# Two match buffers in layer 1 of a graph attention kernel, with other counts of one-hot and weighted-row buffers

## The chip, the cores and the metric

The kernel runs on one core of one Trainium2 chip. A core has a matrix engine (TensorE, PE in the profile, with its weight loads shown as PEld), three engines for element-wise work (VectorE or DVE, ScalarE or ACT, GpSimd or POOL) and a queue engine for transfers (SyncE or SP). The metric is the device time of one execution in microseconds (us); lower is better.

## The reference, cut to what matters

A pre-normalised residual block around a two-layer graph attention network, on 6250 nodes and 100000 edges that are sorted by destination. A loop from each node to itself is added to the edges.

```python
def gat_conv(x, src, dst, W, a_src, a_dst, bias, heads):
    h = (x @ W).reshape(n, heads, -1)
    alpha_s = (h * a_src[None]).sum(-1)
    alpha_d = (h * a_dst[None]).sum(-1)
    e = leaky_relu(alpha_s[src] + alpha_d[dst], 0.2)
    e = exp(e - segment_max(e, dst)[dst])
    alpha = e / (segment_sum(e, dst)[dst] + 1e-16)
    return segment_sum(h[src] * alpha[:, :, None], dst).reshape(n, -1) + bias

h = relu(layernorm(x))                          # 6250 x 768
h = relu(gat_conv(h, src, dst, W1, ..., heads=4))   # 256 features
h = relu(gat_conv(h, src, dst, W2, ..., heads=1))   # 256 features
return x + relu(h @ Wm1 + bm1) @ Wm2 + bm2      # 768 features
```

## The kernel before, in words

**Stages.** Nodes are cut into NT = 49 tiles of 128, edges into 784 tiles of 128 (782 of them with real edges). A first stage normalises x and forms the features of layer 1, one node tile after another; each row (268 numbers: four heads of 64 features and a one, and eight exponentials of the scores) stays in SBUF as `kept[t]` and is also stored to a table in DRAM. Then the edges of layer 1 are worked through, and then those of layer 2, both by the function `layer_edges`. The work after layer 2 (the two dense layers and the residual) is woven into layer 2's loop.

**The loop over groups.** `layer_edges` runs over NG = 196 groups of four edge tiles. The order on every engine is written by hand: each engine runs its own instructions in the order in which the Python code issues them, and waits on semaphores where it must. In group g of layer 1 stand, in this order:

- `gather(g + 8)`: POOL issues one indirect DMA for each of the four tiles (L652). It brings the 128 source rows of the tile into half of a buffer `G`, which holds a pair of tiles. There are 20 such buffers, taken in turn.
- `pair(g, 0)`: DVE forms the weights of a pair in PSUM (`factors`, L730 and L740), and multiplies the gathered rows by them into a buffer `hw` (L742). That is the last read of `G`. PE then multiplies the one-hot matrix `hot` of each tile with `hw` and adds up in PSUM (`o_ps`, L754), two groups to one sum.
- `make_hot(g + 1)`: DVE writes the one-hot matrices of the next group (L680) in a buffer of the pool `eg`.
- in every fourth group pieces of node work, masks and their products with the prepared numbers `win` (L698).
- the matches, see below; then `pair(g, 1)`, and in every second group `take_sum`, in which DVE takes a finished `o_ps` of groups up to g - 4 (L771).

**The matches.** The edges' first rows are needed while the table is still being stored. For 23 pairs of tiles (list `SOON`) the gather ran early, against the part of the table that was there; rows of later nodes are put in afterwards by a product. `soon_hits` has DVE compare the 128 source numbers of a tile with the last m node tiles, m from 2 to 20 (`soon_hit`, 128 x 128m, L379). `soon_missing` has PE multiply them with the rows `kept` (m products, each two records in the profile, L389). `soon_out` has ACT copy the result from PSUM (L395), and `soon_whole` adds it to the row. There are 46 of these, k = 0 to 45: the hits of k stand in group 8i + 1 for k = 2i and in group 8i + 5 for k = 2i + 1, the product two groups after for even k and one after for odd k. Before the change all 46 share one buffer, since the pool `pre1` has one buffer for each name.

**Buffers that bind the engines.** `hot` has 5 buffers, one for each group. `hw` has 10 in layer 1, one for each pair of tiles. `o_ps` has 3 in PSUM.

**Preparing.** `prepare` runs once ahead of each layer: from the scores of all nodes it forms `win` and `own`, with seven arrays in between (`rho`, `parts`, `r1`, `r2`, `e1`, `e2`, `v`). In layer 1 it takes them from the pool `pre1`, which stays open for the whole layer.

Of the kernel before, what the change touches and what calls it, by code (L numbers as in the profile page):

```python
# [10 lines left out]
F32 = mybir.dt.float32  # L11
BF16 = mybir.dt.bfloat16
# [5 lines left out]
P = 128  # L18
# [9 lines left out]
NT = -(-N // P)  # L28
NQ = 4 * NT
TPG = 4  # L30
NG = NQ
# [24 lines left out]
SOON_FROM, SOON_HELD = min(SOON), 16  # L56
# [14 lines left out]
def kernel(  # L71
# [266 lines left out]
    soon_G, soon_of, soon_p, soon_hit, soon_m = {}, {}, {}, {}, {}  # L338
# [34 lines left out]
    def soon_hits(pool, k):  # L373

        i, t = divmod(k, 2)
        if i < len(SOON):
            m = NT - SOON[i]
            soon_hit[k] = pool.tile([P, NT - SOON_FROM, P], F32, name="soon_hit")
            nc.vector.tensor_tensor(  # L379
                soon_hit[k][:, :m],  # L380
                soon_of[i][:, t * P:(t + 1) * P].unsqueeze(1).to_broadcast([P, m, P]),
                nid_ps[:, SOON[i]:].unsqueeze(2).to_broadcast([P, m, P]), ALU.is_equal)
# [178 lines left out]

    def prepare(wk, layer, H):

        s, d = sd[layer][:, :, :H], sd[layer][:, :, H:]
        rho = wk.tile([P, NT, H], F32, name="rho")
        nc.scalar.activation(rho, d, AF.Exp, scale=SLOPE - 1.0)
        parts = wk.tile([P, NT, H, 3], BF16, name="parts")
        nc.vector.tensor_copy(parts[:, :, :, 0], rho)
        r1 = wk.tile([P, NT, H], F32, name="r1")
        nc.vector.tensor_sub(r1, rho, parts[:, :, :, 0])  # L570
        nc.vector.tensor_copy(parts[:, :, :, 1], r1)
        r2 = wk.tile([P, NT, H], F32, name="r2")
        nc.vector.tensor_sub(r2, r1, parts[:, :, :, 1])
        nc.vector.tensor_copy(parts[:, :, :, 2], r2)

        win = wk.tile([P, NG + 4, 3 * H], BF16, name="win")
        pv = parts.rearrange("p n h k -> p n (h k)").unsqueeze(2)
        for q in range(4):
            r = slice(32 * q, 32 * q + 32)
            to = win[r, q:q + NG].rearrange("p (n j) k -> p n j k", j=4)  # L580
            of = pv[r].to_broadcast([32, NT, 4, 3 * H])
            if q % 2:
                nc.scalar.activation(to, of, AF.Copy)
            else:
                nc.vector.tensor_copy(to, of)
        nc.vector.memset(win[64:96, 0:2], 0.0)
        nc.vector.memset(win[96:128, 0:3], 0.0)
        nc.vector.memset(win[0:32, NG:NG + 4], 0.0)
        e1 = wk.tile([P, NT, H], F32, name="e1")
        nc.scalar.activation(e1, s, AF.Exp)  # L590
        e2 = wk.tile([P, NT, H], F32, name="e2")
        nc.scalar.activation(e2, s, AF.Exp, scale=SLOPE)
        v = wk.tile([P, NT, H], F32, name="v")
        nc.vector.tensor_mul(v, e2, rho)
        own = wk.tile([P, NT, H], F32, name="own")
        nc.vector.tensor_max(own, v, e1)
        nc.vector.tensor_reduce(flags[:, layer - 1:layer], sd[layer].rearrange("p n k -> p (n k)"),
                                AX.X, ALU.max, apply_absolute_value=True)
        return SimpleNamespace(win=win, own=own)
# [24 lines left out]
    def layer_edges(layer, H, node, pre, matched, pre_pool):  # L624
# [1 line left out]


        C = HID // H
        with tc.tile_pool(name=f"eg{layer}", bufs=5) as eg, \
                tc.tile_pool(name=f"hw{layer}", bufs=10 if layer == 1 else 14) as hwp, \  # L630
                tc.tile_pool(name=f"sum{layer}", bufs=4) as sums, \
                tc.tile_pool(name=f"sm{layer}", bufs=4) as sm:
            G, hot, e_ps, o_ps = {}, {}, {}, {}
# [231 lines left out]
            for g in range(NG):  # L865
# [39 lines left out]
                if layer == 1:  # L905
                    for i, at in enumerate(SOON_GROUP):
                        for k, hits_at in ((2 * i, at - 10), (2 * i + 1, at - 6)):
                            if g == hits_at + 3 + (k % 2 == 0):
                                soon_out(sm, k)
                            if g == at - 1:  # L910
                                soon_whole(G, k)
                            if g == hits_at:
                                soon_hits(pre_pool, k)
                            if g == hits_at + 1 + (k % 2 == 0):
                                soon_missing(k)
                        if g == at - 13:
                            soon_sources(pre_pool, i)
# [41 lines left out]
    with tc.tile_pool(name="w2p", bufs=1) as wp, tc.tile_pool(name="wk2", bufs=2) as wk:  # L959
# [51 lines left out]
        with tc.tile_pool(name="pre1", bufs=1) as pre:  # L1011
            pre1 = prepare(pre, 1, 4)
            layer_edges(1, 4, Node1(), pre1,
                        lambda: scores_in(ps, w2, *w2_in, KH, 1, "parts", 1), pre)


    with tc.tile_pool(name="wmp", bufs=1) as wp, tc.tile_pool(name="x3", bufs=4) as xp, \
# [10 lines left out]
        def matched():  # L1028

            vars(pre2).update(vars(prepare(pre, 2, 1)))  # L1030
            nc.scalar.dma_start(wm1, Wm1.rearrange("(k p) f -> p k f", p=P))
            nc.scalar.dma_start(wm2, Wm2.rearrange("(k p) f -> p k f", p=P))
            with nc.allow_non_contiguous_dma(reason="256 numbers"):
                nc.scalar.dma_start(bm1c, bm1.rearrange("(k p) -> p k", p=P))
            nc.scalar.dma_start(bm2r, bm2_d)
            nc.vector.memset(ones_r, 1.0)
# [120 lines left out]
        for stage in range(2):  # L1157
            first_hits(pre, 2, stage)
        layer_edges(2, 1, Node2(), pre2, matched, pre)

    edges_stack.close()
# [310 lines left out]
```

## Time and profile before

| what | value |
|---|---|
| median of 3 runs (lowest, highest) | 2555.83 us (2548.58, 2555.97) |
| the profiled execution's own time, and its span | 2560.77 us, 2559.0 us |
| first stage, 0 to 185 us of the span | PE busy 151.19, DVE 121.57, POOL 86.99 us |
| layer 1, 185 to 1345 us | PE 791.57, DVE 720.89, ACT 154.09, POOL 701.70 us |
| between the layers, 1345 to 1436 us | PE 50.35, DVE 43.22, POOL 38.37 us |
| layer 2, 1436 us to the end | PE 792.12, DVE 507.75, POOL 705.50 us |
| mean granted PE clock | 0.793 |
| mean duration of a gather (L652), of a `soon_hit` (L379), of `hw` in layer 1 (L742), of `hot` (L680) | 956, 1640, 695, 682 ns |

Busy time of an engine is the sum of the durations of its instructions; waiting for a semaphore is not in it. PE and PEld overlap, and the ends of matmuls are modelled. The page puts idle time down to what ended it: "remote" or "another core or an unknown queue" is an event for which the profile knows no instruction, and "issue" is time for which it knows no wait. With one core there is no other core, so both leave something untold. L numbers are lines of the kernel before; in the kernel after they are 5 to 7 higher from `prepare` on.

### The profile page before, as it was taken

How to read it: one execution, taken by the hardware profiler on the slowest of the kernel's cores; microseconds unless marked ns; L12 is line 12 of the kernel's file. 1: busy time of each engine (PE TensorE's matmuls, PEld its weight loads, DVE VectorE, ACT ScalarE, POOL GpSimd, SP SyncE). 2: the span in 40 equal slices, each digit the busy share in tenths (PEclk: the TensorE clock that was granted, in tenths of full speed). 3: DMA queues.
4: the chain of work that ended last, by engine and by line, in shares of the span. 5: the costliest groups of instructions: out<-in, count | busy, mean ns of one | idle time of the engine just before them, and what ended most of it. 6: DMA issues, size and time to landing. Idle time of an engine off the chain costs nothing.

```text
span 2559.0 us, 26651 instructions
## 1 busy us (share of the span) xinstructions
PE 1785.2 (70%) x7728; PEld 1282.6 (50%) x7729; DVE 1393.4 (54%) x4195; ACT 442.2 (17%) x1368; POOL 1532.6 (60%) x1666
## 2 busy tenths in 40 slices
PE   9952758667768667767766566676767767776677
PEld 7741546555546445545554344454444444444445
DVE  7742566666667667666666444444444434444444
ACT  6640111111111111111112011111111111111112
POOL 5257465565666666666554566666666666666661
PEclk9985778788778778878878677777878777777778
DMA  9986345545545555555444445545554454545542
GB/s 353 334 272 218 104 136 144 151 131 147 156 134 155 147 142 160 138 155 157 127 117 122 126 121 157 148 137 153 155 154 148 137 154 139 157 145 153 150 148 78
DMA packets 167326, 400.35 MB, mean 156 GB/s; under 512 B 36631, under 2 KB 54254, under 8 KB 167174
## 3 DMA queue, kind: packets, MB, share of 16 engines
q0 software_dynamic: 75072, 211.10, 31.0%
q1 hardware_dynamic: 90732, 185.99, 21.2%
q10 hardware_dynamic: 1370, 1.48, 0.2%
q8 instruction: 65, 1.06, 0.2%
q14 instruction: 87, 0.71, 0.1%
HBM read 333.87 MB, written 64.56 MB: 156 GB/s over the span
## 4 chain that ended last, share of the span: by engine, by line
PE 40%; issue 24%; DVE 15%; another core or an unknown queue 11%; POOL 5%; DMA 4%; ACT 1%; SPq 0%; DVEq 0%; POOLq 0%; ACTq 0%
PE o_ps L754 20%; PE y_ps L1124 6%; POOL G L652 5%; PE missing L389 5%; PE h_ps L452 4%; DVE hw L742 3%; DMA G<-table,src_i 3%; DVE hot L680 3%; DVE factors L740 2%; DVE factors L730 2%; DVE acc L771 1%; PE tp L1114 1%; DVE hw L737 1%; PE e_parts L698 1%
## 5 line engine op out<-in xcount | busy, mean ns | idle before, releaser
L652 POOL DMA_INDIRECT G<-table,src_i x1507 | 1440.7, 956 | 851.8 <-issue 376.3
L754 PE MATMUL o_ps<-G,hw 128*128 128x258 f32 x1564 | 525.2, 462 | 231.3 <-issue 187.3
L754 PE MATMUL o_ps<-hw,hot 128*128 128x260 f32 x1564 | 476.0, 441 | 161.1 <-issue 125.3
L754 PEld LDWEIGHTS o_ps<-G,hw 128*128 128x128 f32 x1564 | 350.6, 231 | 375.9 <-issue 279.7
L754 PEld LDWEIGHTS o_ps<-hw,hot 128*128 128x128 f32 x1564 | 327.1, 217 | 271.5 <-issue 164.4
L389 PE MATMUL missing<-kept,soon_hit 128*128 128x268 f32 x1028 | 265.2, 406 | 71.1 <-issue 70.1
L737 DVE TENSOR_SCALAR hw<-iota_ps,dcol,w 128x128 f32<-128x128 f32 x782 | 284.9, 406 | 16.3 <-DVE w L733 2.0
L742 DVE TENSOR_TENSOR hw<-G,factors 128x520 f32<-128x520 f32 x391 | 271.9, 695 | 22.0 <-DVE factors L740 6.4
L780 ACT ACTIVATE sum<-acc 32x260 f32<-32x260 f32 (+1 forms) x384 | 160.0, 417 | 689.5 <-DVE acc L771 263.5
L389 PEld LDWEIGHTS missing<-kept,soon_hit 128*128 128x128 f32 x1028 | 201.5, 198 | 123.2 <-issue 88.7
L1128 DVE TENSOR_TENSOR y<-y_ps,xt 128x384 f32<-128x384 f32 (+1 forms) x98 | 54.5, 556 | 271.1 <-PE o_ps L754 91.8
L1124 PE MATMUL y_ps<-wm,mT 128*128 128x384 f32 x392 | 181.5, 593 | 13.0 <-ACT mT L1119 8.7
L680 DVE TENSOR_TENSOR hot<-iota_ps,dcol 128x512 f32<-128x512 f32 x196 | 133.6, 682 | 104.2 <-remote 97.2
L379 DVE TENSOR_TENSOR soon_hit<-soon_of,iota_ps 128x1408 f32<-128x1408 int32 (+18 forms) x46 | 75.4, 1640 | 210.2 <-remote 140.2
L452 PE MATMUL h_ps<-w,r 128*128 128x264 f32 (+1 forms) x588 | 141.3, 395 | 19.4 <-ACT r L442 10.8
L698 PE MATMUL e_parts<-win,mask 128*128 128x12 bf16 (+1 forms) x1564 | 70.2, 168 | 116.7 <-issue 116.0
L452 PEld LDWEIGHTS h_ps<-w,r 128*128 128x128 f32 x588 | 110.5, 195 | 42.9 <-ACT r L442 12.9
L730 DVE TENSOR_TENSOR factors<-G,factors 128x8 f32<-128x8 f32 (+1 forms) x782 | 125.0, 160 | 7.1 <-DVE acc L771 2.6
L698 PEld LDWEIGHTS <-mask 128*128 128x128 bf16 x1564 | 62.7, 99 | 130.8 <-issue 122.0
L1124 PEld LDWEIGHTS y_ps<-wm,mT 128*128 128x128 f32 x392 | 77.8, 221 | 88.2 <-issue 48.1
L1119 ACT ACTIVATE mT<-tp,bm1c 128x128 f32<-128x128 f32 x98 | 30.6, 363 | 508.5 <-PE o_ps L754 305.7
L771 DVE SCALAR_TENSOR_TENSOR acc<-acc,keep,o_ps 128x260 f32<-128x260 f32 (+1 forms) x192 | 91.3, 475 | 11.7 <-PE o_ps L754 8.3
(418 smaller groups left out, 1281.4 us busy)
## 6 DMA issues: line engine op xcount, KB each, us to landing
xt<-in_x SPq DMA_DIRECT2D x96, 384.0 KB
drow<-dmod_d SPq DMA_DIRECT2D x49, 512.0 KB
mask_d<-mask SPq DMA_DIRECT2D x97, 256.0 KB
mask<-mask_d SPq DMA_DIRECT2D x97, 256.0 KB
G<-table,src_i POOLq DMA_INDIRECT x1507
xTt<-in_xT SPq DMA_DIRECT2D x49, 384.0 KB
out<-y SPq DMA_DIRECT2D x48, 384.0 KB
table<-kept SPq DMA_DIRECT2D x49, 134.0 KB
```

The lines of the kernel that those rows point to most:

```text
L389: nc.tensor.matmul(soon_p[k], hit[:, T - there], kept[T], start=(T == there), stop=(T == NT - 1))
L452: nc.tensor.matmul(h_ps[:, :n], r[:, k], w1[:, k, :n], start=(k == 0), stop=(k == KI - 1))
L652: nc.gpsimd.indirect_dma_start(out=G[k // 2][:, k % 2], out_offset=None, in_=table[layer], in_offset=bass.IndirectOffsetOnAxis(ap=src_i[:, ...
L680: nc.vector.tensor_tensor(hot[g][:, T[0]:T[0] + n], iota_ps.unsqueeze(1).to_broadcast([P, n, P]), dcol[:, k:k + n].unsqueeze(2).to_broadca ...
L698: nc.tensor.matmul(parts[t][:, at + k], m[:, k * P:(k + 1) * P], pre.win[:, 2 * u + 2], start=True, stop=True)
L730: nc.vector.tensor_mul(v, e2, rho)
L737: nc.vector.tensor_scalar(hw[:, t], iota_ps, dcol[:, k:k + 1], w[:, t], ALU.is_equal, ALU.mult)
L742: nc.vector.tensor_mul(hw, Gp[:, :, :RW[1]].rearrange("p t (h c) -> p t h c", h=H), w.unsqueeze(3).to_broadcast([P, 2, H, C + 1]))
L754: nc.tensor.matmul(o_ps[u], l, r[:, :RW[layer]], start=(g % 2 == 0 and k == 0), stop=(g % 2 == 1 and k == tiles(g)[-1]))
L771: nc.vector.scalar_tensor_tensor(acc, run[0], keep[:, u % 2:u % 2 + 1], o_ps.pop(u), ALU.mult, ALU.add)
L780: nc.scalar.activation(done[t][r], acc[r], AF.Copy)
L1124: nc.tensor.matmul(y_ps, mT[:, j], wm2[:, j, s * half:(s + 1) * half], start=False, stop=(j == KH - 1))
```

## The change

`soon_hit` gets two buffers in turn. `hot` gets 6 buffers instead of 5 (the pool `eg` is opened with 6 in layer 2 too, where nothing is taken from it). `hw` gets 8 in layer 1 instead of 10. `prepare` takes `win` and `own` from the pool that stays, and everything else from a pool of its own that is closed when `prepare` ends, so its room goes to the pools opened after it.

```diff
-            soon_hit[k] = pool.tile([P, NT - SOON_FROM, P], F32, name="soon_hit")
+            soon_hit[k] = pool.tile([P, NT - SOON_FROM, P], F32, name="soon_hit", bufs=2)
...
     def prepare(wk, layer, H):
 
+        win = wk.tile([P, NG + 4, 3 * H], BF16, name="win")
+        own = wk.tile([P, NT, H], F32, name="own")
+        with tc.tile_pool(name=f"prep{layer}", bufs=1) as tmp:
+            return prepared(tmp, layer, H, win, own)
+
+    def prepared(wk, layer, H, win, own):
+
         s, d = sd[layer][:, :, :H], sd[layer][:, :, H:]
...
-        win = wk.tile([P, NG + 4, 3 * H], BF16, name="win")
...
-        own = wk.tile([P, NT, H], F32, name="own")
...
-        with tc.tile_pool(name=f"eg{layer}", bufs=5) as eg, \
-                tc.tile_pool(name=f"hw{layer}", bufs=10 if layer == 1 else 14) as hwp, \
+        with tc.tile_pool(name=f"eg{layer}", bufs=6) as eg, \
+                tc.tile_pool(name=f"hw{layer}", bufs=8 if layer == 1 else 14) as hwp, \
```

In bytes of a partition, a `soon_hit` takes 10240, a `hot` 2048, an `hw` 2080, and the seven arrays of `prepare` in layer 1 together 5880.

The order of the instructions on every engine is the same in both kernels. What differs is the semaphores that some wait for: in the kernel after, no `soon_hit` waits for PE, 158 of the `hot` no longer do, and 362 of the `hw` of layer 1 wait for PE where they waited for DVE alone. `rho` at the head of `prepare` waits for other queues.

## The prediction

> **What bounds the kernel now.** I read the page's head, then the windows by stage, then who waits in layer 1, then the timelines of POOL, DVE and PE over a few periods.
>
> ```profile
> span 2559.0 us, 26651 instructions
> ...
> 185.00:1345.00 1160.00, 791.57 (x3567) 600.04 (x3568) 720.89 (x1860) 154.09 (x535) 701.70 (x731) 0.80 0.52 147
> ...
> 1436.00:2559.00 1123.00, 792.12 (x3292) 528.39 (x3291) 507.75 (x1907) 165.52 (x437) 705.50 (x742) 0.77 0.48 143
> ```
>
> Columns: stretch, length, busy us (and count) of PE, PEld, DVE, ACT, POOL, then granted clock, DMA share, GB/s. The change can act in layer 1 alone. No engine is near full there, so waits set the time. The waits in layer 1:
>
> ```profile
> DVE soon_hit L379 <- remote: 140.2, 18, 9.8
> DVE hot L680 <- remote: 97.2, 15, 18.9
> DVE soon_hit L379 <- PE missing L389: 47.8, 5, 23.7
> DVE soon_hit L379 <- PE o_ps L754: 21.6, 4, 7.6
> ...
> POOL G L652 <- DVE hw L742: 196.8, 57, 15.0
> ...
> PE o_ps L754 <- DVE hw L742: 15.6, 20, 2.2
> ```
>
> Each line is us in total, times, the longest. DVE stands 210 us in front of soon_hit (140.2 + 47.8 + 21.6), POOL 197 us for hw to free a G. That looks like 200 us to be had. The timeline says otherwise. POOL, then DVE, around one such wait:
>
> ```profile
> 629.61 0.94 POOL L652 DMA_INDIRECT G<-table,src_i  x1 [0.30 <-issue]
> 636.61 0.94 POOL L652 DMA_INDIRECT G<-table,src_i  x1 [6.05 <-DVE hw L742]
> ...
> 623.00 0.48 DVE L669 TENSOR_SCALAR mask<-drow,pidx 128x1024 bf16<-128x1024 bf16 x1
> 633.22 0.69 DVE L379 TENSOR_TENSOR soon_hit<-soon_of,iota_ps 128x512 f32<-128x512 int32 x1 [9.73 <-remote]
> 634.23 0.70 DVE L742 TENSOR_TENSOR hw<-G,factors 128x520 f32<-128x520 f32 x1
> ...
> 626.12 0.17 PE L698 MATMUL e_parts<-win,mask 128*128 128x12 bf16 x1 [0.63 <-issue]
> 626.82 0.18 PE L698 MATMUL e_parts<-win,mask 128*128 128x12 bf16 x1 [0.53 <-issue]
> 628.92 0.17 PE L698 MATMUL e_parts<-win,mask 128*128 128x12 bf16 x1 [1.92 <-issue]
> ```
>
> The product that the buffer waited for had left PE's timeline 1.7 us before DVE arrived. DVE went on at 633.22, when PE did: from 625.1 to 633.1 PE starts a matmul only every 0.7, 1.4 or 2.1 us, where sixteen of these take 0.55 us elsewhere. I call this a crawl. By the POOL timeline, crawls belong to gathers: this one starts 14.5 us into a run of 16 gathers without a pause (610.6 to 630.6) and ends 2.6 us after its last. In layer 1 nearly every run of 12 or more has one, from 11 to 18 us on; runs of 10 or fewer have almost none. What makes it is open. A crawl ends because POOL runs out of free G buffers, DVE frees none, and POOL pauses.
>
> So a cycle is: some 14 us of gathers with PE and DVE at speed, a crawl in which only POOL gets on, a pause. From 300 to 1326 us POOL issues 646 gathers, one per 1.255 us when nothing stops it (956 ns and 0.30 of issue): 811 us. The other 215 us are its pauses, and those are what this stage can give back.
>
> **The change part by part.**
>
> *soon_hit's second buffer.* I went through the 51 pauses over 0.8 us from 300 to 1326 us and noted what DVE does first after the crawl. In 23 it is the waiting soon_hit: they are 5.68 us long on average (130.6 in all) and hold 39.3 us of soon_hit, as it delays the hw that frees a G. In 14 it is the waiting hot: 5.37 us on average. The other 14 are 1.5 us on average. With two buffers DVE does soon_hit when it arrives, about 1.5 us ahead of the crawl. At the most a pause loses its soon_hit and the two small steps behind it (0.20 + 0.21 us from start to start), as L742 would wait next: 39.3 + 23 x 0.41 = 49 us. At the least nothing, if PE's groups end later than the crawl. The nearest row is the 14 pauses whose wait is already for PE's groups: less the hot itself (0.60 from start to start) they are 4.77 us, 0.91 shorter, so 23 x 0.91 = 21 us. I take 21.
>
> Beside the product, PE must be able to follow. It waits for DVE 15.6 us by the row above, and small gaps of 0.1 to 0.8 us in its timeline make another 32: some 48 us of room in all.
>
> *hot 6 for 5, hw 8 for 10.* Before, hot(x + 1) needs group x - 4 off PE; after, pair p of group x needs pair p of group x - 4. Both hold DVE four groups ahead. Behind the wait stand the rest of the group on DVE, then PE and POOL. Gain: hot is done before the wait, 14 x 0.60 = 8 us. Loss: when PE is held in the first half of a group, one pair less is freed ahead of the stall, two gathers of POOL's run, 2.5 us x 14 = 35 us if never made up; it is freed first at the restart. I take 0 and keep both ends.
>
> *Semaphores.* 362 hw get a second wait, a separate instruction of 0.021 us: at the most 7.6 us. Where one stands in such a place now (hw, then factors L730, start to start 0.729 us) it costs the same as where none does (hw, then L717, 0.729). I take 0.
>
> *Preparing.* The same instructions in the same order; rho waits for other queues, but its scores come last anyway. Ahead of each layer this is under 1 us. 0.
>
> *What is given back.* A shorter pause may bring the next crawl earlier. Layer 2 has the rows: after pauses of 2 to 3.5 us its crawls begin 6 to 12 us into a run, against some 14.5 us after 5.7 in layer 1. About 1.2 us sooner per us of pause makes 1.1 us less at speed in each of the 37 cycles. With 4.7 us of gathers a group and one pause per some five groups, a cycle that loses a third of a group costs about 0.07 us a group: 188 groups, 13 us at the most. I take half, 6.
>
> Sum: -21 + 0 + 0 + 0 + 6 = -15. The profiled execution took 2560.77 us, with 1.8 us outside its span; less 15 that is 2545.8. The median of the runs is 4.9 lower: 2540.8, so 2541.
>
> **A rule against the row.** The Trainium skill, "TensorE: Matmul & The Clock Gate", Part 1 (the HAM clock gate), says that PE falls to half its clock after an idle window of about 3.4 us and is back after as long a busy one. Read by that, the crawls are PE gone cold while it waits for DVE, and feeding PE earlier cures them. The row:
>
> ```profile
> 653.68 0.39 PE L389 MATMUL missing<-kept,soon_hit 128*128 128x268 f32 x1 [0.60 <-issue]
> 655.78 0.60 PE L389 MATMUL missing<-kept,soon_hit 128*128 128x268 f32 x1 [1.71 <-issue]
> 657.17 0.61 PE L389 MATMUL missing<-kept,soon_hit 128*128 128x268 f32 x1 [0.79 <-issue]
> 659.97 0.60 PE L389 MATMUL missing<-kept,soon_hit 128*128 128x268 f32 x1 [2.19 <-issue]
> ```
>
> PE had work queued and took 2.1 us a product, where 0.22 is full speed; after crawls at 0.5 granted it is 0.44. So the half clock fits the rule, the crawl doesn't. Gaps on the 0.7 us grid hold 286 us of layer 1, the half clock 64. By the rule up to 64 us would come on top of the 15 (2477); by the row none.
>
> **Rivals.**
>
> *The whole wait goes.* Taking 210 us at its word gives 2346. Against it: the wait ends with the crawl, not with the product. Its likelier form is the full 49 + 8 us, 2499.
>
> *PE takes over, no change.* PE uses its time outside crawls for all but some 48 us. If longer crawls or its own groups eat the gain, DVE stands at hw where it stood at soon_hit, and the time stays within 8 us: 2548 to 2564. For it: hot already waits 97 us in layer 1.
>
> *Slower: short crawls become long.* DVE, no longer stopped, frees more G ahead of the crawl, so POOL runs longer and the crawl lasts. Crawls headed by soon_hit are now mostly 8 us, those headed by hot 20. PE needs some 640 us outside crawls in this stage, so layer 1 grows once crawl time grows by more than PE's room of 48: from 4 of the 23 turned from 8 to 20 us (12 each). Six make 72 - 48 = +24 (2580), eight +48 (2604). Against it: POOL works in a crawl, and freed pairs are progress.
>
> *It doesn't do what it says* is out: no soon_hit waits for PE any more.
>
> **How the numbers follow.** No change is within 0.3%, some 8 us, about what a measurement can tell. Faster 0.52 (2541 with its own range 2499 to 2548), no change 0.18, slower 0.30. The range runs from 2504, which leaves out the full gain, to 2576, which leaves out seven crawls and more turned.
>
> **What would show it.** Right: no time before soon_hit in the waits; pauses after crawls near 4.8 us; POOL's wait for hw in layer 1 down by some 20 us; layer 2 as before. The rivals: soon_hit's 210 us reappearing at hw with POOL's pauses as long as now (no change), or more 20 us crawls (slower). Wrong altogether if crawls start at another place of a run of gathers than now, or layer 2 moves.

## The result and the profile after

The change took 0.6% off: 2542.35 us (median of 20 runs) beside 2556.19 us for the kernel before on the same chip, ratio 0.9938, 95% interval 0.9921 to 0.9956. The prediction said 2541. The profiled execution took 2548.37 us, its span 2546.6, against 2560.77 and 2559.0 before. Later comparisons, on other chips, show that this gain is not found everywhere: on three others the kernel before takes some 2100 us, and on the two of them where the full change ran as well there is no difference.

The head of the page after and the two groups whose waits the change was to move (busy us, mean ns of one, then the idle time ahead of them):

```profile
span 2546.6 us, 26991 instructions
...
L747 DVE TENSOR_TENSOR hw<-G,factors 128x520 f32<-128x520 f32 x391 | 272.2, 696 | 167.5 <-remote 103.0
...
L685 DVE TENSOR_TENSOR hot<-iota_ps,dcol 128x512 f32<-128x512 f32 x196 | 133.4, 681 | 0.0
```

`soon_hit` has left the list of groups with idle time, `hot` waits for nothing any more (104.2 us before), and `hw` (L747, the old L742) has 167.5 us ahead of it over the whole span, 133.8 of them in layer 1 against 9.1 before. The windows by stage, with the columns as before:

```profile
185.00:1345.00 1160.00, 784.42 (x3616) 607.24 (x3617) 736.66 (x1909) 161.10 (x552) 695.15 (x731) 0.79 0.51 148
...
1436.00:2546.00 1110.00, 780.26 (x3238) 520.73 (x3237) 495.48 (x1858) 165.09 (x436) 693.97 (x730) 0.77 0.48 143
```

DVE is a little busier in the window of layer 1 than it was (736.66 us against 720.89), and no engine is near full. Comparing the start of each gather in the two traces shows where the time went: the 120th starts 2 us earlier than before, the 200th 16, the 240th 7, the 700th 24, the 760th (near the end of layer 1) 17, and from there to the end the lead stays between 15 and 18. So the gain is made in layer 1, in ups and downs, and layer 2 runs as before.

The prediction looked for the gain in POOL's pauses. From the 100th to the 760th gather (1059 us before, 1043 after) the pauses over 0.8 us add up to 236.6 us before and 226.8 after, 10 us less. The other 7 us are in the gathers themselves: they take 635.0 us before and 627.9 after, and 69 of them are longer than 1.0 us before, 34 after. Why, no run shows. This is one trace of each kernel, and the 20 runs of each spread over 27 and 28 us, so the split is a reading of two traces and no more. The waits in layer 1, DVE's, then POOL's after, then two of POOL's before (us in all, times, the longest):

```profile
DVE hw L747 <- remote: 103.0, 29, 7.0
...
DVE G L401 <- ACT soon_m L395: 27.2, 6, 5.0
...
DVE all__9155 L984 <- issue: 21.4, 1, 21.4
DVE hw L747 <- PE o_ps L759: 12.3, 10, 3.1
DVE all__5339 L984 <- ACT sum L785: 11.8, 1, 11.8
```

```profile
POOL G L657 <- DVE hw L747: 164.9, 44, 18.7
POOL G L657 <- DVE factors L735: 63.5, 47, 6.4
POOL G L657 <- DVE factors L745: 14.7, 14, 4.9
```

```profile
POOL G L652 <- DVE factors L730: 37.9, 28, 5.8
POOL G L652 <- DVE factors L740: 34.1, 41, 6.7
```

The 210 us at `soon_hit` are gone, and 125 us at `hw` and 108 us at `all_` (L984) have come: added up over all its lines, `all_` waits 135.0 us in place of 27.4. It is the add that closes a node tile (`mine` plus `sum`), and nothing in the change touches it. POOL's wait for `hw` fell from 196.8 to 164.9; its waits for the two lines of `factors` moved from one to the other and rose by 6 us in sum. ACT's wait at `soon_m`, the copy of a product, was long before (first line) and is longer now:

```profile
ACT soon_m L395 <- remote: 209.2, 20, 13.7
```

```profile
ACT soon_m L395 <- remote: 233.6, 15, 22.4
```

The timeline of one slow stretch (what the prediction calls a crawl) shows how `all_` comes into it:

```profile
862.91 2.13 DVE L379 TENSOR_TENSOR soon_hit<-soon_of,iota_ps 128x1920 f32<-128x1920 int32 x1
...
870.78 0.17 PE L703 MATMUL e_parts<-win,mask 128*128 128x12 bf16 x1 [2.62 <-issue]
...
873.59 0.17 PE L703 MATMUL e_parts<-win,mask 128*128 128x12 bf16 x1 [2.64 <-issue]
...
881.41 0.39 ACT L395 ACTIVATE soon_m<-missing 128x268 f32<-128x268 f32 x1 [22.00 <-remote]
881.83 0.86 ACT L785 ACTIVATE sum<-acc 32x260 f32<-32x260 f32 x2
882.27 0.43 DVE L984 TENSOR_TENSOR all__6605<-mine,sum 128x260 f32<-128x260 f32 x1 [11.41 <-ACT sum L785]
```

`soon_hit` runs at 862.91 without a wait, just ahead of the slow stretch (865 to 881), as the change intends. But ACT, which also runs in order, stands at `soon_m`, the copy of the product before, for 22 us, until PE is back at speed. The sums stand behind `soon_m` on ACT, `all_` waits for a sum on DVE, and the `hw` that free `G` stand behind `all_`. POOL pauses from 877.7 to 885.7, 8 us, longer than the 5.68 that pauses headed by `soon_hit` took. In a pause like this one nothing is left of the second buffer's gain. Taking as the head the DVE instruction that waited longest, `all_` heads 12 of the pauses over 0.8 us from 300 to 1326 us (8.0 us on average) and `hw` 22 (3.0 us).

### The profile page after: what moved, and what is told of

It is laid out like the page before. It is cut to its first block, busy times and chain, and to the rows that moved or that the text cites. A ratio compares the mean times of both kernels' runs of the same rounds, so it can differ in the third digit from the quotient of the medians.

```text
span 2546.6 us, 26991 instructions
## 1 busy us (share of the span) xinstructions
PE 1767.1 (69%) x7728; PEld 1284.8 (50%) x7729; DVE 1391.6 (55%) x4195; ACT 445.0 (17%) x1368; POOL 1525.2 (60%) x1666
## 4 chain that ended last, share of the span: by engine, by line
PE 52%; issue 24%; DVE 10%; another core or an unknown queue 8%; POOL 2%; DMA 2%; ACT 2%; DVEq 0%; ACTq 0%; POOLq 0%
PE o_ps L759 27%; PE missing L389 8%; PE y_ps L1129 6%; PE h_ps L452 4%; POOL G L657 2%; PE tp L1119 2%; PE e_parts L703 2%; DMA G<-table,src_i 1%; DVE hw L742 1%; PE h_ps L1007 1%; DVE hw L747 1%; DVE hot L685 1%; PE y_ps L1068 1%; DVE factors L735 1%
## 5 line engine op out<-in xcount | busy, mean ns | idle before, releaser
L759 PE MATMUL o_ps<-hw,hot 128*128 128x260 f32 x1564 | 455.7, 431 | 126.9 <-issue 104.5
L747 DVE TENSOR_TENSOR hw<-G,factors 128x520 f32<-128x520 f32 x391 | 272.2, 696 | 167.5 <-remote 103.0
L389 PE MATMUL missing<-kept,soon_hit 128*128 128x268 f32 x1028 | 271.9, 416 | 65.3 <-issue 38.6
L742 DVE TENSOR_SCALAR hw<-iota_ps,dcol,w 128x128 f32<-128x128 f32 x782 | 284.9, 406 | 16.4 <-DVE w L738 2.2
L389 PEld LDWEIGHTS missing<-kept,soon_hit 128*128 128x128 f32 x1028 | 207.6, 205 | 116.9 <-issue 71.4
L960 ACT ACTIVATE rT<-tp,bT 128x128 f32<-128x128 f32 x196 | 61.2, 363 | 195.3 <-remote 81.0
```

The lines of the kernel that those rows point to most:

```text
L389: nc.tensor.matmul(soon_p[k], hit[:, T - there], kept[T], start=(T == there), stop=(T == NT - 1))
L742: nc.vector.tensor_scalar(hw[:, t], iota_ps, dcol[:, k:k + 1], w[:, t], ALU.is_equal, ALU.mult)
L747: nc.vector.tensor_mul(hw, Gp[:, :, :RW[1]].rearrange("p t (h c) -> p t h c", h=H), w.unsqueeze(3).to_broadcast([P, 2, H, C + 1]))
L759: nc.tensor.matmul(o_ps[u], l, r[:, :RW[layer]], start=(g % 2 == 0 and k == 0), stop=(g % 2 == 1 and k == tiles(g)[-1]))
```

## The experiments

The comparisons were made on four chips, here B, C, D and E, in this order and each used once (A is the chip of the first comparison; the results don't name it, and it may be B). The kernel before took 2587.61, 2098.43, 2101.42 and 2098.81 us on B, C, D and E. "Ratio" is always to the kernel before on the same chip. Differences in us are worked out from the ratio and its 95% interval, which rest on all runs; two medians can differ from them by a few us. There is no trace of the kernel before on B, so traces from B are set beside the one from A.

### One part at a time (chip B)

The second buffer alone: hot and hw as before.

```diff
-        with tc.tile_pool(name=f"eg{layer}", bufs=6) as eg, \
-                tc.tile_pool(name=f"hw{layer}", bufs=8 if layer == 1 else 14) as hwp, \
+        with tc.tile_pool(name=f"eg{layer}", bufs=5) as eg, \
+                tc.tile_pool(name=f"hw{layer}", bufs=10 if layer == 1 else 14) as hwp, \
```

> Only soon_hit's second buffer (and the room from the preparing numbers that pays for it); hot keeps 5 buffers, hw keeps 10. Here no hw carries a second wait; 182 hot carry one on PE, as 160 did before. Theory (the gain is the second buffer's, and the 362 second waits of the full change cost 0.07 us each, 25 us of VectorE, about half of it on the path): 2530 us, that is 26 below before and 12 below the full change; waits at soon_hit gone, L740 to L742 start to start back at 0.208 us. Rival (the counts 6 and 8 carry part of the gain, since hot no longer waits for PE): 2545 to 2550, with 80 to 100 us of waits at hot.

Measured: 2583.37 us, ratio 0.9969 (0.9944 to 0.9993), 8 us below before (the medians are 4 apart); the theory wanted 26. L745 to L747 is back at 0.208 us from start to start, as expected. DVE's largest wait in layer 1 is now this one, where the full change has none:

```profile
DVE hot L685 <- remote: 143.3, 25, 9.2
```

With its other lines, `hot` waits 174.5 us, and `all_` 144.9. So what `soon_hit` no longer waits for, the next instruction that needs PE waits for. Counted as above, `hot` heads 24 pauses here, 4.8 us on average, about as long as those headed by `hot` before (12, 5.0 us); but `all_` heads another 10 of 9.1 us.

The counts alone: `hot` 6 and `hw` 8, one `soon_hit`.

```diff
-            soon_hit[k] = pool.tile([P, NT - SOON_FROM, P], F32, name="soon_hit", bufs=2)
+            soon_hit[k] = pool.tile([P, NT - SOON_FROM, P], F32, name="soon_hit")
```

> Only hot 6 and hw 8; soon_hit keeps its one buffer. 270 hw carry a second wait. Theory: soon_hit's 210 us of waits stay, 270 x 0.07 = 19 us are added on VectorE, part of it on the path: 2560 us (4 over before). Rival (the counts bring the gain): 2545.

Measured: 2594.91 us, ratio 1.003 (1.0005 to 1.0054), 8 us slower than before (interval 1 to 14, which holds the theory's 4). The trace has 228 second waits, not the expected 270. DVE's first waits in layer 1:

```profile
DVE soon_hit L379 <- remote: 188.2, 25, 10.7
DVE soon_hit L379 <- PE missing L389: 74.2, 5, 43.2
DVE hw L747 <- remote: 28.9, 8, 5.6
```

`hot` has stopped waiting and `soon_hit` waits more than before (274.5 us in all, against 210.2). The counts bring nothing by themselves. On chip B the two parts add up to no change, while the full change gained 0.6% on chip A. The full change as it stands was not run on B; the two runs of the next section bear on whether the parts help each other.

### Taking the new wait away (chip B)

The full change, with `soon_out` moved behind the sums. For odd k this also puts the copy one group later than before, into the group just ahead of the add that reads it.

```diff
-                            if g == hits_at + 3 + (k % 2 == 0):
-                                soon_out(sm, k)
...
+                if layer == 1:
+                    for i, at in enumerate(SOON_GROUP):
+                        for k, out_at in ((2 * i, at - 6), (2 * i + 1, at - 2)):
+                            if g == out_at:
+                                soon_out(sm, k)
```

> The full change, and soon_out (the product's copy by ScalarE, soon_m, and what follows it) issued at the end of the group, behind the sums that stood behind it. Theory (part of the gain is given back as VectorE's add all_ waits for ScalarE's sum, which stands behind soon_m, 136.8 us against 28.6 before): all_'s waits fall to 30 to 50 us, ten pauses of POOL of 8 us become pauses of 5 to 6, 2525 us. Rival (PE's slow stretch sets the end of the pause whoever heads it): the wait moves to another line, 2540 to 2545.

Measured: 2573.09 us, ratio 0.9953 (0.993 to 0.9976), 12 us below before; the theory wanted 31, the rival 11 to 16. The move did what it was to do: `all_` waits 35.4 us in place of 135.0. The waits went elsewhere:

```profile
DVE hw L747 <- remote: 88.1, 30, 8.7
DVE G L401 <- ACT soon_m L395: 83.8, 14, 8.2
DVE factors L745 <- remote: 51.5, 18, 3.4
```

`G` (L401), the add that needs `soon_m`, waits 83.8 us where it waited 27.2 on chip A. All 14 of these waits belong to odd k, so the move itself has a part in them, and this run alone doesn't show that the slow stretch merely found another head.

The same move on the second buffer alone:

> Both: only soon_hit's second buffer, hot 5 and hw 10, and soon_out at the end of the group. Theory: the gains add, 2530 for the second buffer alone less 15: 2515 us. Rival: whichever heads the pause, it ends with PE's slow stretch: 2530 to 2545.

Measured: 2578.49 us, ratio 0.9969 (0.9949 to 0.9988), the same as without the move: 8 us below before, where the theory wanted 41 and the rival 11 to 26. Here `G` waits 12.7 us in all, and nearly everything has gathered at `hot`:

```profile
DVE hot L685 <- remote: 271.4, 30, 37.8
```

`all_` fell from 144.9 us to 31.3, `hot` rose from 174.5 to 302.5, and the time is the same. This is the clean case of a wait that only moves. One table says it for the six traces. Each entry is the sum of DVE's waits from 185 to 1345 us:

| kernel (chip) | all waits | at soon_hit | at hot | at hw | at all_ | ratio |
|---|---|---|---|---|---|---|
| before (A) | 407 | 210 | 104 | 9 | 27 | 1 |
| full change (A) | 369 | 0 | 0 | 134 | 135 | 0.9938 |
| second buffer alone (B) | 413 | 0 | 175 | 13 | 145 | 0.9969 |
| counts alone (B) | 409 | 275 | 0 | 44 | 7 | 1.003 |
| full change, late copy (B) | 385 | 0 | 0 | 113 | 35 | 0.9953 |
| second buffer, late copy (B) | 414 | 0 | 303 | 12 | 31 | 0.9969 |

The heads change completely; the sum keeps between 369 and 414. Adding up the distances between PE's starts that lie within 0.05 us of 0.7, 1.4 or 2.1 us, from 185 to 1345 us, gives 298, 250, 317, 286, 254 and 316 us in the table's order. They outlast every arrangement of buffers (the prediction's 286 is another count of the same gaps). Both sums are lowest in the two kernels with the whole change, which also have the lowest ratios.

On whether the parts help each other: with the late copy on chip B, adding the counts to the second buffer took the ratio from 0.9969 to 0.9953 (the intervals overlap), where the counts alone cost 0.3%. So it seems that their cost alone is not simply added to the second buffer's gain; the difference is only just clear of the noise, and why is open.

### The counts of gathered rows, and a chip without slow stretches (chips C, D, E)

The prediction tied the slow stretches to unbroken runs of gathers. Fewer buffers `G` cut the runs.

```diff
-AHEAD = 8
+AHEAD = 4
...
-SOON_FROM, SOON_HELD = min(SOON), 16
+SOON_FROM, SOON_HELD = min(SOON), 8
```

> The full change with gathers issued 6 groups ahead in place of 8: 16 buffers of gathered rows in place of 20 (SOON_HELD 12). Theory (PE's slow stretch begins 10 to 16 us into an unbroken run of gathers and ends about 3 us after it; the run goes on until the free buffers are used up): runs of 22 gathers become runs of 16 to 18, slow stretches shorten by 5 us each, the 0.7 us gaps fall from 294 us to 200, ratio 0.97. Rival (the slow stretch has another cause and the lookahead covers it): POOL pauses sooner in each, ratio 1.00 to 1.01.

> The same with 4 groups ahead: 12 buffers (SOON_HELD 8). Theory: runs of 12 to 14 gathers, hardly any slow stretch in layer 1 (the 0.7 us gaps under 80 us), ratio 0.95. Rival: the slow stretches stay as long, POOL pauses for all of each, 20 to 40 pauses of 10 us more, ratio 1.03 to 1.08.

Beside them ran the full change again, and the full change with `hot` at 5.

> The full change again, beside the others. Ratio to before 0.994, as in its first comparison; waits at soon_hit gone, VectorE's waits at hw about 100 us.

> The full change with hot back at 5 buffers (hw stays at 8). 181 hw carry a second wait and 182 hot one on PE. Theory (soon_hit's buffer and the sixth hot each bring part: with the soon_hit wait gone, VectorE stands at hot next, 143 us where only soon_hit's buffer was given): 143 us of waits at hot come back, ratio 0.997 to 0.998. Rival (the head of the pause doesn't matter, PE's slow stretch sets its end): ratio 0.994, as the full change.

Measured on chip C, where the kernel before took 2098.43 us: full change 1.0003 (0.9995 to 1.0012), `hot` 5 and `hw` 8 0.9998 (0.9989 to 1.0008), 6 groups ahead 1.0016 (1.0007 to 1.0024), 4 groups ahead 1.0023 (1.0014 to 1.0031). None of these expectations was made for such a chip, and none came about, but for the number of one rival: 1.00 to 1.01 with 6 groups ahead. Its reason, POOL pausing in each slow stretch, has no place in a trace whose gathers run 754 in a row. To see what is different there, the kernel before was run for its own trace:

> The kernel before itself, one look, to have its trace beside the others on this chip. Theory (the waits at soon_hit are made by PE's slow stretches, and these come on some chips and not on others): if it takes about 2098 us, VectorE's waits at soon_hit are under 10 us and the gathers run in one unbroken run; if it takes 2550 to 2590, they are 200 to 260 us. Rival (the second buffer takes away a wait of the program's order, on any chip): 50 us or more at soon_hit at 2098 us too.

It took 2103.28 us on chip D, and the theory's first case came about. DVE's largest wait, its wait at `soon_hit` and POOL's largest, from 185 to 1100 us, which is layer 1 there:

```profile
DVE factors L730 <- DMA G<-table,src_i: 122.7, 90, 5.0
...
DVE soon_hit L379 <- PE missing L389: 4.2, 4, 1.6
```

```profile
POOL G L652 <- issue: 146.4, 480, 0.3
```

4.2 us at `soon_hit` in place of 210, and no wait of POOL longer than 0.3: its gathers run 762 in a row, one per 1.25 us. DVE waits for the gathered rows, not POOL for DVE. The full change on chip C reads the same, with nothing at `soon_hit` and

```profile
DVE factors L735 <- DMA G<-table,src_i: 105.2, 72, 3.2
```

The windows of the two, kernel before first:

```profile
185.00:1100.00 915.00, 752.87 (x3617) 581.12 (x3619) 742.63 (x1922) 158.65 (x569) 694.22 (x725) 0.92 0.65 183
```

```profile
185.00:1100.00 915.00, 752.09 (x3623) 576.03 (x3624) 740.82 (x1923) 158.50 (x569) 693.42 (x724) 0.93 0.65 183
```

The layer's work, which takes 1160 us on chip A, is done in 915, at the same durations of a gather (medians of 946 ns on A, 949 before on D, 946 after on C). The 100th to the 760th gather take 834 us in both kernels; on chip A they took 1059 and 1043. The distances near 0.7, 1.4 or 2.1 us, added up as above but from 185 to 1100 us, come to 32 us on D and 76 on C.

> The full change with 12 buffers of gathered rows in place of 20. Where the kernel before takes 2550 to 2590: theory (an unbroken run of gathers brings the slow stretch on, after 10 to 16 us of it): hardly any slow stretch in layer 1, ratio 0.95. Rival (the slow stretch comes anyway, and a shorter lookahead only stops POOL sooner): ratio 1.02 to 1.08. Where it takes 2098: as in the run before, 1.002.

> The full change once more, for a chip on which the kernel before takes 2550 to 2590. There: theory (its gain is made by PE's slow stretches): ratio 0.993 to 0.996. Rival (the gain of the first comparison was that chip's alone): 0.999 to 1.001. On a chip with 2100 both say 1.000.

> Again 12 buffers of gathered rows in place of 20. On a chip on which the kernel before takes 2550 to 2590: theory (an unbroken run of gathers brings the slow stretch on after 10 to 16 us): hardly any slow stretch in layer 1, ratio 0.95. Rival (the slow stretch comes anyway, and POOL stops sooner in each): ratio 1.02 to 1.08. On a chip with 2100: 1.002 to 1.004, as before.

Measured: 4 groups ahead 1.0035 (1.0022 to 1.0047) on D and 1.0024 (1.0015 to 1.0033) on E; the full change 1.0005 (0.9996 to 1.0014) on E, all close to what was expected for a chip with 2100 us. None of these runs was on a chip with slow stretches, so whether shorter runs of gathers avoid them is open. The 12 buffers cost 5 to 7 us on C, D and E: 4 groups of lookahead nearly cover a gather on such a chip, and POOL has no pause over 0.8 us in layer 1 with them either.

## Why the prediction was right, point by point

**What bounds the kernel: right for its chip.** Waits set the time of layer 1, and their end is PE's slow stretch, not the product that `soon_hit` waits for. That `soon_hit`'s 210 us were worth little was the step that mattered. Had they been worth their length, the time would have been 2346; every arrangement of the buffers that was run moved it by under 0.7%. On D, without slow stretches, the same program waits 4.2 us there.

**soon_hit's second buffer, -21: over-sized.** Alone it gave 8 us (interval 2 to 14) on chip B. The step took the 14 pauses headed by `hot` as the model of what comes next, with 4.77 us for a pause. Where `hot` came next, in the run with the second buffer alone, the pauses were about as long as in the row that it took (4.8 us with the `hot` itself, where the prediction had 5.37). What the step left out is `all_`: in the trace after, eight pauses of 7.4 to 8.0 us are headed by `all_`, which waits behind ACT's `soon_m`. The prediction looked at what stands behind the waiting instruction on DVE, and not at ACT, whose `soon_m` already waited 209.2 us ("remote") before. The late copy on the second buffer alone speaks for a new head and not a new cause: with `all_` cured, `hot` waited instead, and the time stayed.

**hot 6 for 5, hw 8 for 10, taken as 0: within its ends.** Alone 8 us slower on chip B (1 to 14), inside the -8 to +35 given. That run also carries 228 second waits (16 us of DVE by the next point), so it isn't the counts' own share alone.

**Semaphores, taken as 0, at the most 7.6: wrong.** L740 to L742 was 0.208 us from start to start; with a second wait, L745 to L747 is 0.277 to 0.280 in 315 of the 362 cases of the trace after, and never less; in the others `hw` really waited. Without one it is 0.207 to 0.210 in every trace, unless something is waited for. That is 0.070 us each, 25 us of DVE. The step priced the wait by its own record (0.021 us) and by a place behind an instruction of 0.695 us (`hw`), where nothing of it showed. What it costs in time is another matter. On the chips without slow stretches DVE's wait for gathered rows is 17.5 us shorter with the full change, 105.2 us on C against 122.7 before on D, and on C and E the time stayed within 0.2%: there it is covered.

**Preparing, 0; what is given back, +6.** Nothing shows at `prepare`. The giving back was foreseen in kind: a slow stretch that begins sooner, by 1.1 us a cycle. Counting its begin as the first PE start that is followed by at most six in 4 us, in runs of 12 or more gathers from 300 to 1326 us, it came 12.7 us into the run on average before (30 stretches) and 10.4 after (26), 2.3 us sooner. The prediction's reason, a shorter pause ahead, doesn't show: within neither trace do the two go clearly together (correlation 0.36 and -0.12). What this took back can't be put in a number of its own.

Of what the prediction wanted to see, three things are there: no time at `soon_hit`, layer 2 as before, and POOL's wait for `hw` down, by 32 us where some 20 were wanted, though its pauses fell by 10 only. The pauses headed by `soon_hit` are gone, but not for pauses near 4.8 us: those headed by `hw` take 3.0, those headed by `all_` 8.0. And one of its signs of being wrong altogether, slow stretches at another place of a run, is there by the 2.3 us above, though in the direction of its own term.

So the sum of -15 met -13.8 (2542.35 less 2556.19) with one term too large, one too small, and a wait that was not foreseen. That it met it within 2 us is luck: on chip B its one large term gave 8 us alone and its zero for the counts cost 8, and on A, in the pauses where it looked for the gain only 10 us are found. What it had right is that most of the wait is worth nothing, and why. **The rivals:** the full gain (2499) and the slower case (2580 and up) did not come. "The time stays within 8 us, DVE stands at `hw` where it stood at `soon_hit`" came half true on chip A: DVE stands there 134 us. On C and E no change is the result, but for a reason that the rival did not name: there the gathers set the time and there is no wait to take away.

**"In layer 1 nearly every run of 12 or more gathers has a slow stretch": true on A and B, not enough by itself.** Counted as above, 30 of 31 such runs have one before, all 26 after, and all of them in the four traces of B. On C, D and E runs of 748 and 762 gathers pass without one.

**The rule on the clock.** The prediction set aside the Trainium skill, "TensorE: Matmul & The Clock Gate", Part 1, by which PE falls to half its clock after some 3.4 us of idling. The rows after agree. The window ahead of the slow stretch above, and the stretch:

```profile
850.00:865.00 15.00, 14.85 (x73) 12.55 (x72) 14.00 (x35) 3.50 (x13) 11.20 (x12) 1.00 0.69 207
...
865.00:881.00 16.00, 1.35 (x8) 0.71 (x7) 5.28 (x17) 0.00 (x0) 9.70 (x11) 0.60 0.41 111
```

The granted clock is 1.00 up to the stretch and falls to 0.5 at 868.2 us in the trace's record of it, 3 us after the stretch began; it is back at 1.00 at 885.2, 4 us after PE is at speed again (881.3). The gate follows the stretch, as the rule would have it for an idle PE, and does not start it. The 1.35 us of PE in 16 are not half speed either. That C, D and E grant a higher mean clock (0.89 against 0.79) would then be an effect of the missing stretches, by the same rule; no run here tries it apart.

What makes a slow stretch stays open. It goes with the chip or with the time: the same program has them on A and B and not on C, D and E, but each was used once, A and B before the others, and what else ran on a chip isn't on record. Meanwhile the gathers' durations and their distance of 1.25 us are the same. On A and B it also goes with gathers: the first 100 us, without gathers and with more transfer (over 330 GB/s against some 150), have none.

## What to carry to other kernels

A long wait in the list is worth what is left when it ends: look for the event that ends it, and for every in-order engine that the same event holds. When each of several stalls ends with one event, moving buffers among them changes the names in the list of waits and little else. And a trace is of one chip at one time: before a stall of 200 us is worked on, look whether it is there on a second.

## What the runs showed of the hardware

- C, D and E ran the kernel before in 2098 to 2101 us, A and B in 2556 and 2588. From the 100th to the 760th gather the difference is 226 us (1059.5 on A, 833.9 on D), and POOL's pauses over 0.8 us come to 237 us on A and none on D. Most of them follow stretches in which PE starts a matmul only every 0.7, 1.4 or 2.1 us.
- In such a stretch ACT went on with a product's copy (`soon_m`, 881.41) 18 us after the product's last record ended (863.0). Whether the event was late, or is raised by a matmul that stood behind in PE's order, the profile doesn't tell ("remote").
- A second semaphore to wait for put 0.070 us ahead of a DVE instruction even where neither was really waited for (0.278 against 0.208 us from the start of the one before it, an instruction of 0.17 us; the same on every chip).
